# Turning gathered token slices in pairs on two row groups of the matmul engine, and four changes of order beside it

## The chip, the cores and the metric

The kernel runs on one core of a Trainium2 chip. That core has a matmul engine (PE, with its own row for weight loads, PEld), a vector engine (DVE), a scalar engine (ACT), a general engine (POOL) and a queue engine (SP). The metric is the device time of one execution in microseconds (us). All times here are of that one core.

## The reference

Two layers follow each other on x, 16 batches of 128 tokens with 512 features.

```
x = x + attention(layernorm(x), ctx, ctx)      # 32 query heads, 8 key heads, 16 wide, 128 keys
h = layernorm(x)                               # 2048 tokens of 512
tidx, tw = gate(h)                             # 32 experts in 8 groups; best 4 groups, best 8 experts
routed = sum over the 8 chosen experts e of tw[e] * (silu(h @ w1[e].T) * (h @ w3[e].T)) @ w2[e].T
shared = (silu(h @ sw1.T) * (h @ sw3.T)) @ sw2.T      # inner width 256, as each expert
x = x + routed + shared
```

All arithmetic on tokens is fp32.

## The kernel before, in words

The program is one stream of instructions per engine, in an order that is written out by hand: within each engine instructions run in the order in which the Python code emits them, and waits between engines follow from the data and from the memory banks that the tiles share. There are four stages.

**Attention** (lines 272 to 630). There are 32 items, one for each batch and each parity of key heads. An item's `scores` (line 423) are matmuls of 32 rows in four row groups of PE, `values` (line 442) are matmuls of 32 columns in four column groups, and `added` (line 457) turns the result back and adds it to x on POOL. `queries(b)` (line 411) turns one batch's queries on PE and copies them on DVE. Work beside the items hangs on two tables, `head` and `tail`, by item number: layernorm statistics on DVE, reciprocal roots on POOL (`first_rstd`), the masked keys of the next four batches on POOL (`keys`, lines 344 to 350), their values (`fixed_values`, `values_of`). `gate_parts` and `gate_sums` compute the gate's logits. At the end the first of the shared expert's up matmuls fill gaps on PE (`shared_up`, line 246). One shared up is eight matmuls of 512 columns into two PSUM banks: one is read by ACT's silu (line 261), the other by a product on DVE (line 264). An fp32 matmul appears as two records in the trace, a transpose as one.

**Routing** (`route`, line 1033). DVE works out from the logits which experts each token takes (`sel`, line 1129). PE then counts tokens for each expert and ranks them (lines 1137 to 1216). PE has shared up matmuls as cover: `up_matmuls(20)` ahead of the choice, 4 and 9 behind the ranks. Three products of the cover, named `product`, `product0` and `product1`, sit at chosen places in DVE's order. The cover's accumulators come from the pool `ps_gu`, [...].

**The table of tokens** (lines 1289 to 1329). For each of the 16 batches DVE, POOL and ACT build one-hot tiles (`hr`, `hq`, `ht`; two buffers each) and PE multiplies them into `tok`, the list of token numbers for 138 slices of 128 places. Between them PE runs the rest of the shared ups, two matmuls for each batch, and the shared expert's 16 `shared_down`s (two fp32 matmuls each); DVE adds each of these to x (`add_down`) in the `meanwhile` part of the next batches, after that batch's one-hot tiles.

**The experts** (lines 1334 to 1513). The 138 slices are laid one after another, expert after expert, and cut into 52 pieces of at most 512 places. `gather(j)` fetches slice j from DRAM with an indirect DMA that POOL issues, five slices ahead. `turn(j)` (line 1368) transposes the slice on PE, four transposes of 128 x 128 into one bank of `ps_x` (two buffers), and ACT copies it into `xnT` (line 1374). Each piece has four steps. A step is one `up` (four fp32 matmuls, line 1395), then some turns of slices that the next piece needs, then some `down`s (two fp32 matmuls, line 1449; where a slice holds the end of one expert and the start of the next it is done in column groups of 32 or 64). After `down(j)` ACT scales the result (line 1458) and POOL issues an indirect DMA that adds it to the output (line 1421). The loop at lines 1505 to 1509 spreads turns and downs over the four steps:

```
left = 4 - step
for _ in range(-(-turns_left // left)):
    turn_next()
    turns_left -= 1
for _ in range(-(-len(downs_left) // left)):
    down(downs_left.pop(0))
```

Of the kernel before, what the change touches and what calls it, by code (L numbers as in the profile page):

```python
# [9 lines left out]
F32 = mybir.dt.float32  # L10
# [5 lines left out]
PSUM = bass.MemoryType.PSUM  # L16
DRAM = bass.MemoryType.DRAM

P = 128
# [27 lines left out]
def tile_xattn_moe(  # L47
# [15 lines left out]
    nc = tc.nc  # L63
    B, S, D = x.shape
    E, _, ND, I = w1.shape
    NI = I // P
    KV = D // HD // G
    NT = B
    NTB = NT // 4
# [5 lines left out]
    NS = begins[E] // P  # L75
# [6 lines left out]
    ident = const.tile([P, P], F32, name="ident")  # L82
# [189 lines left out]
    def attention_small():  # L272


        with ExitStack() as ph:
# [23 lines left out]
            for half, eng in enumerate((nc.sync, nc.scalar)):  # L299
                rows_of_half = slice(half * P // 2, (half + 1) * P // 2)  # L300
# [217 lines left out]
            def at_head(n, f, *a):  # L518
                head.setdefault(n, []).append((f, a))
# [17 lines left out]
            for b in range(3, B):  # L537
                at_head(2 * b - 3, rows_of, b)

            at_head(1, fixed_values, 1, nc.gpsimd)  # L540
            at_head(1, keys, 1)
            at_head(2, values_of, 1)
            for k in range(2, NTB):
                at_head(8 * k - 7, keys, k)
                at_head(8 * k - 6, values_of, k)
# [27 lines left out]
            for n in range(N):  # L573
                for f, a in head.get(n, ()):
                    f(*a)

                scores(*items[n])
                if n > 0:
                    values(*items[n - 1])
                if n in parts:  # L580
                    gate_parts(parts[n])
                if (n == 1 or n % 2 == 0 and n > 0) and n // 2 + 1 < B:
                    queries(n // 2 + 1)
                keep_warm(FILL.get(n, 0))
                if n in sums:
                    gate_sums(sums[n])
                if n > 1:
                    added(*items[n - 2])
                if n in turned:
                    gate_turn(turned[n], ps_tr)  # L590
                for f, a in tail.get(n, ()):
                    f(*a)
# [365 lines left out]
    def experts(ups, in_order, later, products):  # L958
# [33 lines left out]
        )  # L992
        token2 = wp.tile([P, E - 1], I32, name="token2")
        ps_y = ctx.enter_context(tc.tile_pool(name="ps_y", bufs=2, space=PSUM))
        ps_gu = ctx.enter_context(tc.tile_pool(name="ps_gu", bufs=2, space=PSUM))
        ps_rt = early.enter_context(tc.tile_pool(name="ps_rt", bufs=1, space=PSUM))
        ps_sm = early.enter_context(tc.tile_pool(name="ps_sm", bufs=2, space=PSUM))
        oh = early.enter_context(tc.tile_pool(name="oh", bufs=2))
# [34 lines left out]
        def route():  # L1033
# [70 lines left out]
            for t in range(NT):  # L1104
                nc.vector.max(t8[:, t, :], ms[:, t, :])
                nc.vector.match_replace(rp[:, t, :], t8[:, t, :], ms[:, t, :], LOWEST)
                if t == NT // 2:
                    product1()
                if t == NT // 2 + 1:


                    ranked_p = new([E, 4], "ranked_p")
                    diag = new([E, E], "diag")
                    for i in range(4):
                        nc.vector.scalar_tensor_tensor(
                            diag,
                            ranked[:, i // 2, i % 2 : i % 2 + E],
                            1.0,
                            ident[0:E, 0:E],
                            ALU.mult,  # L1120
                            ALU.mult,
                            accum_out=ranked_p[:, i : i + 1],
                        )
                    rise = new([E, 2], "rise", F16)
                    nc.vector.tensor_tensor(
                        rise, ranked_p[:, 1::2], ranked_p[:, 0::2], ALU.subtract
                    )
# [34 lines left out]
            nc.vector.tensor_scalar(less, size, size_p, None, ALU.is_lt)  # L1162
            sm = new([P, NT], "sm")
            nc.vector.tensor_reduce(sm, comb, AX.X, ALU.add)

            rank = ps_rt.tile([P, NT, E], F32, tag="rank", name="rank")
            nc.tensor.matmul(rank, lhsT=before, rhs=sel, start=True, stop=False)
# [124 lines left out]
        for b in range(NT):  # L1292

            meanwhile = later + held
            held = list(products)
            if b > NT - NTB:
                meanwhile += held
                held.clear()
            later.clear()
            products.clear()  # L1300
            slot_tokens(
                b,
                sr,
                sq,
                slice_q,
                tok,
                oh,
                lambda k: nc.gpsimd if k % 4 == 3 else nc.vector,
                meanwhile,
            )  # L1310
            if b == 2:
                weights()
            if b == 6:
                flags()
            up_matmuls(2)

            for _ in range(b % 2 if b < NT - NTB else 2 if b < NT - 1 else 1):
                shared_down(next(downs))
        finish_tokens(token, tok, oh)
        for f in later + held:  # L1320
# [11 lines left out]


        ps_gu2 = ctx.enter_context(tc.tile_pool(name="ps_gu2", bufs=2, space=PSUM))
        ps_x = ctx.enter_context(tc.tile_pool(name="ps_x", bufs=2, space=PSUM))
        tp = ctx.enter_context(tc.tile_pool(name="tp", bufs=3))
        pieces = []
        for k in range(E):
# [26 lines left out]
            )  # L1365
            xg[j] = t

        def turn(j):
            t = xg.pop(j)
            tr = ps_x.tile([P, ND, P], F32, tag="trx", name="trx")  # L1370
            for d in range(ND):
                nc.tensor.transpose(tr[:, d, :], t[:, ts(d, P)], ident)  # L1372
            for n, a, b, col in parts(j):
                nc.scalar.copy(xnT[n % NTB][:, :, col : col + b - a], tr[:, :, a:b])  # L1374

            ks = [pieces[n][0] for n, *_ in parts(j)]
            by = owner[:, ks[0] : ks[0] + 1] if ks[0] == ks[-1] else owner2[:, ks[0] : ks[0] + 1]
            own = tp.tile([P, E], F32, tag="own", name="own")
            nc.vector.scalar_tensor_tensor(  # L1379
                own, expert, by, t[:, D:], ALU.is_equal, ALU.mult, accum_out=wt[:, j : j + 1]  # L1380
            )
            if ks[0] != ks[-1]:
                k = ks[0]
                nc.vector.tensor_tensor(
                    token2[:, k : k + 1], token[:, j : j + 1], outside[:, k : k + 1], ALU.add
                )
# [91 lines left out]

        def turn_next():
            nonlocal n_turned, n_gathered  # L1480
            if n_gathered < NS:
                gather(n_gathered)
                n_gathered += 1
            turn(n_turned)
            n_turned += 1

        def slices_of(n):

# [5 lines left out]
        for n in range(len(pieces)):  # L1494
            tasks = []
            whole = slices_of(n - 1)[1] if n else 0
            needed = slices_of(n + 1)[0] if n + 1 < len(pieces) else NS
            downs_left = list(range(n_down, whole))
            turns_left = needed - n_turned
            n_down = whole  # L1500
            banks = {}
            for step in range(4):
                up(n, step // 2, step % 2, banks)
# [6 lines that stand above are left out]
# [75 lines left out]
```

## Time and profile before

| | us |
|---|---|
| median of 3 runs | 1013.0 (1012.27 to 1016.13) |
| profiled execution, its own time | 1011.92 |
| its span | 1010.1 |
| PE busy in the span | 987.3 (98%) |
| PE weight loads | 574.8 |
| POOL busy | 512.7 |
| ACT busy | 325.8 |
| DVE busy | 253.3 |
| 552 transposes of gathered slices on PE (line 1372) | 82.9, 273 ns mean of one |
| 150 copies of turned slices on ACT (line 1374) | 81.5, 551 ns mean of one |

The span runs from the first to the last instruction of the core; some 1.8 us of the execution's own time lie around it. The busy time of PE counts a matmul from its start to its modelled end. Matmuls overlap, so the mean of one is longer than the distance from one start to the next, and the distance is what one costs. The granted clock of PE is 0.996 over the span.

### The profile page before, as it was taken

To read this page: it belongs to the slowest core of one execution; us is meant where nothing else is said; L and a number is where in the kernel's file an instruction comes from. 1 tells how busy PE (TensorE), PEld (TensorE's weight loads), DVE (VectorE), ACT (ScalarE), POOL (GpSimd) and SP (SyncE) were. 2 spreads that over 40 slices of the span, in tenths; PEclk is the share of its full clock that TensorE was granted. 3 is DMA by queue.
4 is the path that set the end of the run, shared out by engine and by line. 5 is a ranking of instruction groups with operands and counts; after the bars stand their busy time and mean duration, and the time that the engine had idled before them with its cause. 6 is when DMAs were issued, how large, how long until landed. Compare 5 with 4: busy or idle time off the path is not lost.

```text
span 1010.1 us, 12452 instructions
## 1 busy us (share of the span) xinstructions
PE 987.3 (98%) x4177; PEld 574.8 (57%) x4177; DVE 253.3 (25%) x901; ACT 325.8 (32%) x517; POOL 512.7 (51%) x658
## 2 busy tenths in 40 slices
PE   9999998999999999999999999999999999999996
PEld 5344444547566556676767676767654444444453
DVE  7887668961011000111111111111101000101000
ACT  5666612422222222232323232323232222222221
POOL 5588633754445445554545454545463444554443
PEclk9999999999999999999999999999999999999998
DMA  9011105135666757775757575757575777675643
GB/s 308 8 43 52 54 22 188 52 110 158 158 145 153 160 134 167 167 166 128 188 127 186 127 186 127 187 126 186 129 179 119 169 173 180 142 150 139 124 66 45
DMA packets 59864, 137.06 MB, mean 136 GB/s; under 512 B 12168, under 2 KB 16392, under 8 KB 59792
## 3 DMA queue, kind: packets, MB, share of 16 engines
q0 software_dynamic: 32032, 69.25, 36.3%
q1 hardware_dynamic: 27680, 66.81, 19.9%
q8 instruction: 35, 0.57, 0.2%
q14 instruction: 37, 0.30, 0.1%
q10 hardware_dynamic: 80, 0.13, 0.0%
HBM read 96.71 MB, written 46.73 MB: 142 GB/s over the span
## 4 chain that ended last, share of the span: by engine, by line
PE 76%; POOL 10%; issue 7%; DVE 4%; DMA 2%; ACT 0%; POOLq 0%; DVEq 0%; ACTq 0%
PE gu L1395 44%; PE y L1449 21%; PE trx L1372 6%; PE gu L253 3%; POOL hq L938 2%; POOL out_dram L1421 2%; POOL xn L217 2%; POOL x L474 1%; DMA out_dram<-yw,token 1%; DVE st L91 1%; PE warm L325 1%; POOL kz L350 1%; DVE oTs L454 1%; PE sc L429 1%; POOL h L113 0%
## 5 line engine op out<-in xcount | busy, mean ns | idle before, releaser
L1395 PE MATMUL gu<-xnT,wup 128*128 128x256 f32 (+27 forms) x1664 | 493.2, 445 | 2.4 <-ACT xnT L1374 1.7
L1395 PEld LDWEIGHTS gu<-xnT,wup 128*128 128x128 f32 x1664 | 313.1, 190 | 193.0 <-issue 132.6
L1421 POOL DMA_INDIRECT out_dram<-yw,token x150 | 235.8, 1572 | 357.7 <-ACT yw L1458 258.4
L1449 PE MATMUL y<-wdn,sa 128*128 128x512 f32 (+2 forms) x672 | 260.1, 594 | 0.0
L1406 DVE TENSOR_TENSOR sa<-sl,gu 128x256 f32<-128x256 f32 (+27 forms) x104 | 52.2, 502 | 690.3 <-PE gu L1395 672.0
L1358 POOL DMA_INDIRECT xg<-rows,token x138 | 145.5, 1054 | 48.4 <-issue 33.3
L1458 ACT ACTIVATE yw<-y,wt 128x512 f32<-128x512 f32 x138 | 94.8, 687 | 179.1 <-PE y L1449 153.7
L1449 PEld LDWEIGHTS y<-wdn,sa 128*128 128x128 f32 (+2 forms) x672 | 92.4, 171 | 72.5 <-issue 71.0
L1374 ACT COPY xnT<-trx 128x512 f32<-128x512 f32 (+3 forms) x150 | 81.5, 551 | 141.6 <-PE trx L1372 131.1
L1404 ACT ACTIVATE sl<-gu 128x256 f32<-128x256 f32 (+27 forms) x104 | 46.7, 449 | 240.5 <-PE gu L1395 234.2
L1372 PEld LDWEIGHTS trx<-ident,xg 128*128 128x128 f32 x552 | 69.0, 141 | 36.2 <-issue 24.0
L1372 PE MATMUL trx<-ident,xg 128*128 128x128 f32 x552 | 82.9, 273 | 0.4 <-DMA xg<-rows,token 0.4
L439 ACT ACTIVATE p<-sc 128x1024 f32<-128x1024 f32 x64 | 62.1, 1021 | 29.1 <-PE sc L429 29.1
L253 PE MATMUL gu<-xnT,sup 128*128 128x512 f32 x128 | 59.5, 602 | 2.5 <-DVE sa L264 1.7
L938 POOL TENSOR_SCALAR hq<-slice_q,sq 128x138 f16<-128x138 f16 x32 | 35.2, 1113 | 39.0 <-DVE sq L1242 22.9
L429 PE MATMUL sc<-qT,kz 32*128 32x512 f32 x256 | 41.6, 639 | 1.1 <-DVE qT L420 0.9
L253 PEld LDWEIGHTS gu<-xnT,sup 128*128 128x128 f32 x128 | 22.7, 190 | 26.0 <-issue 20.9
L445 PE MATMUL oT<-p,va 128*32 128x512 f32 x256 | 34.1, 605 | 1.1 <-DVE oTs L454 1.1
L474 POOL TENSOR_TENSOR x<-x,at 128x256 f32<-128x256 f32 x32 | 23.4, 733 | 21.5 <-DVE at L467 21.5
L1379 DVE SCALAR_TENSOR_TENSOR own<-expert,owner,xg 128x32 f32<-128x32 f32 x138 | 31.8, 247 | 1.2 <-DMA xg<-rows,token 1.2
L936 ACT ACTIVATE ht<-hr,token 128x1024 f16<-128x1024 f16 x16 | 18.3, 1147 | 34.4 <-DVE hr L929 34.4
L1276 PE MATMUL y<-sdn,sa 128*128 128x512 f32 x64 | 29.3, 595 | 0.0
(177 smaller groups left out, 467.1 us busy)
## 6 DMA issues: line engine op xcount, KB each, us to landing
wup<-in_w_dram SPq DMA_DIRECT2D x64, 512.0 KB
wdn<-in_w_dram SPq DMA_DIRECT2D x32, 512.0 KB
rows<-xn SPq DMA_DIRECT2D x16, 256.0 KB
out_dram<-x SPq DMA_DIRECT2D x16, 256.0 KB
x<-in_x_dram SPq DMA_DIRECT2D x15, 256.0 KB
out_dram<-yw,token POOLq DMA_INDIRECT x150
xg<-rows,token POOLq DMA_INDIRECT x138
cTs<-in_cT_dram SPq DMA_DIRECT2D x4, 256.0 KB
```

Of the source, the lines that this page charges most:

```text
L253: nc.tensor.matmul(acc, lhsT=sup[:, w, d, ts(i, P)], rhs=xnT[k][:, d, :], start=(d == 0), stop=(d == ND - 1),)
L429: nc.tensor.matmul(scs[j // 2][:, j % 2], lhsT=kzs[b // 4 % 2][rows, b % 4, i, :], rhs=qTs[b][rows], start=True, stop=True, tile_position= ...
L439: nc.scalar.activation(p, sc, AF.Exp, scale=1.0 / HD**0.5)
L938: engine(k).tensor_scalar(hq[:, k, :], tile_q, sq[:, b, k : k + 1], None, ALU.is_equal)
L1358: nc.gpsimd.indirect_dma_start(out=t, out_offset=None, in_=rows[:, :], in_offset=bass.IndirectOffsetOnAxis(ap=token[:, j : j + 1], axis=0) ...
L1372: nc.tensor.transpose(tr[:, d, :], t[:, ts(d, P)], ident)
L1374: nc.scalar.copy(xnT[n % NTB][:, :, col : col + b - a], tr[:, :, a:b])
L1395: nc.tensor.matmul(acc[:, 0:m], lhsT=wup[k % NW][:, w, d, ts(i, P)], rhs=xnT[n % NTB][:, d, 0:m], start=(d == 0), stop=(d == ND - 1),)
L1406: nc.vector.tensor_tensor(acts[n % NTB][:, i, 0:m], banks[2][:, 0:m], acc[:, 0:m], ALU.mult)
L1421: ins = nc.gpsimd.indirect_dma_start(out=flat, out_offset=bass.IndirectOffsetOnAxis(ap=token2[:, k - 1 : k] if a else token[0:b, j : j + 1 ...
L1449: nc.tensor.matmul(y[c0:c1, :], lhsT=acts[n % NTB][:, i, col : col + c1 - c0], rhs=wdn[pieces[n][0] % NW][:, i, :], start=(i == 0), stop=( ...
L1458: nc.scalar.activation(yws[j], y, AF.Copy, scale=wt[:, j : j + 1])
```

## The change

There are five edits.

1. The turn takes two slices. Each slice's 128 rows are taken as two halves of 64. A half is transposed with `tile_position=(0, 0)` or `(64, 0)`: 64 rows of weights by 128 columns, 64 columns moving, so eight transposes for a slice in place of four. The two halves alternate and write to two banks of one `trx` tile, which now has one buffer of two banks. The copy on ACT reads a whole slice from both banks at once; the two parts of a slice that is shared between pieces are copied half by half. `turn_next` gathers two slices and turns two; the number of turns for a piece is halved, rounded up.
2. In the attention, the values and keys of batches 4 to 7 move from items 1 and 2 to items 3, 4 and 5, and `queries(1)` runs ahead of `values` of item 0 instead of behind it.
3. `ps_gu` is taken from the other end of PSUM.
4. In the routing, `product1` moves from the middle of the choice of experts to behind the sums of the weights.
5. In the table, the last four batches get 2, 1, 1 and 0 shared downs in place of 2, 2, 2 and 1, so six are left for behind the table in place of three.

```diff
@@ attention
-            at_head(1, fixed_values, 1, nc.gpsimd)
-            at_head(1, keys, 1)
-            at_head(2, values_of, 1)
+            at_head(3, fixed_values, 1, nc.gpsimd)
+            at_head(4, keys, 1)
+            at_head(5, values_of, 1)
...
                 scores(*items[n])
+                if n == 1:
+                    queries(1)
                 if n > 0:
                     values(*items[n - 1])
...
-                if (n == 1 or n % 2 == 0 and n > 0) and n // 2 + 1 < B:
+                if n % 2 == 0 and 0 < n // 2 < B - 1:
                     queries(n // 2 + 1)
@@ experts
-        ps_gu = ctx.enter_context(tc.tile_pool(name="ps_gu", bufs=2, space=PSUM))
+        ps_gu = ctx.enter_context(tc.tile_pool(name="ps_gu", bufs=2, space=PSUM, side="right"))
@@ route
-                if t == NT // 2:
-                    product1()
...
             nc.vector.tensor_reduce(sm, comb, AX.X, ALU.add)
+            product1()
@@ table
-            for _ in range(b % 2 if b < NT - NTB else 2 if b < NT - 1 else 1):
+            for _ in range(b % 2 if b < NT - NTB else (NT - b) // 2):
                 shared_down(next(downs))
@@ the turn
-        ps_x = ctx.enter_context(tc.tile_pool(name="ps_x", bufs=2, space=PSUM))
+        ps_x = ctx.enter_context(tc.tile_pool(name="ps_x", bufs=1, space=PSUM))
-        def turn(j):
+        H = P // 2
+        def turn(js):
+            tr = ps_x.tile([P, 2, 2, ND, H], F32, tag="trx", name="trx")
+            for s, j in enumerate(js):
+                for d in range(ND):
+                    for h in range(2):
+                        rows_of_half = slice(h * H, (h + 1) * H)
+                        nc.tensor.matmul(
+                            tr[:, h, s, d, :],
+                            lhsT=xg[j][rows_of_half, ts(d, P)],
+                            rhs=ident[rows_of_half, rows_of_half],
+                            start=True,
+                            stop=True,
+                            is_transpose=True,
+                            tile_position=(h * H, 0),
+                        )
+            for s, j in enumerate(js):
+                turned(j, tr[:, :, s])
+        def turned(j, tr):
             t = xg.pop(j)
-            tr = ps_x.tile([P, ND, P], F32, tag="trx", name="trx")
-            for d in range(ND):
-                nc.tensor.transpose(tr[:, d, :], t[:, ts(d, P)], ident)
             for n, a, b, col in parts(j):
-                nc.scalar.copy(xnT[n % NTB][:, :, col : col + b - a], tr[:, :, a:b])
+                if b - a == P:
+                    nc.scalar.copy(
+                        xnT[n % NTB][:, :, col : col + P].rearrange("p d (h t) -> p h d t", h=2), tr
+                    )
+                    continue
+                for h in range(2):
+                    a0, b0 = max(a, h * H), min(b, (h + 1) * H)
+                    if a0 < b0:
+                        nc.scalar.copy(
+                            xnT[n % NTB][:, :, col + a0 - a : col + b0 - a],
+                            tr[:, h, :, a0 - h * H : b0 - h * H],
+                        )
...
         def turn_next():
             nonlocal n_turned, n_gathered
-            if n_gathered < NS:
-                gather(n_gathered)
-                n_gathered += 1
-            turn(n_turned)
-            n_turned += 1
+            js = range(n_turned, min(n_turned + 2, NS))
+            for _ in js:
+                if n_gathered < NS:
+                    gather(n_gathered)
+                    n_gathered += 1
+            turn(js)
+            n_turned += len(js)
...
-            turns_left = needed - n_turned
+            turns_left = -(-(needed - n_turned) // 2)
```

## The prediction

> **What bounds the kernel now.** I read the busy time of the engines by stage first, because the changes lie in four stages. Columns: length, then busy us and count for PE, PEld, DVE, ACT, POOL, the granted clock, DMA share, GB/s.
>
> ```profile
> 0.00:132.00 132.00, 126.14 (x921) 59.89 (x921) 99.59 (x251) 80.16 (x98) 87.66 (x199) 1.00 0.27 93
> 132.00:172.00 40.00, 35.35 (x130) 16.31 (x131) 30.57 (x131) 7.96 (x11) 13.34 (x143) 1.00 0.21 73
> 172.00:228.00 56.00, 56.00 (x240) 28.22 (x239) 45.41 (x127) 17.64 (x17) 34.72 (x32) 1.00 0.32 110
> 228.00:985.00 757.00, 754.23 (x2830) 460.53 (x2829) 76.53 (x390) 215.84 (x385) 367.73 (x278) 1.00 0.66 151
> ```
>
> PE bounds everything. In the experts' 757 us it stands still for 2.8 us, and no other engine is half full, so a cost there is the distance between PE starts. The routing, 132 to 172 us, has 4.65 us without PE; there a wait is worth its length.
>
> The timeline of PE at one turn (start, length, line):
>
> ```profile
> 528.44 0.60 PE L1372 MATMUL trx<-ident,xg 128*128 128x128 f32 x4
> 528.97 1.92 PE L1449 MATMUL y<-wdn,sa 128*32 128x512 f32 x16
> 530.82 0.69 PE L1395 MATMUL gu<-xnT,wup 128*128 128x252 f32 x2
> ```
>
> and at another, where a full-width down follows:
>
> ```profile
> 503.34 0.60 PE L1372 MATMUL trx<-ident,xg 128*128 128x128 f32 x4
> 503.77 1.88 PE L1449 MATMUL y<-wdn,sa 128*128 128x512 f32 x4
> ```
>
> 503.34 to 503.77 is four transposes: 109 ns each, not the 273 ns of the mean row. Two slices cost 8 x 109 = 872 ns. At 528.44 the down in column groups starts 0.53 us after, 92 ns later than 4 x 109: [...] The way back shows it again: 16 records in groups of four are 4 x 429 = 1.72 us, so the down's data has passed at 530.73, and the next up starts at 530.82; its first weights are not loaded ahead either, so its second record comes 317 ns later where 212 is its pace (105 more).
>
> The nearest row for row groups is the scores of attention, 32 rows in four groups. Weight loads, then matmuls:
>
> ```profile
> 65.53 0.20 PEld L429 LDWEIGHTS sc<-qT,kz 32*128 32x128 f32 x4 [0.17 <-issue]
> 65.53 0.71 PE L429 MATMUL sc<-qT,kz 32*128 32x512 f32 x4
> ```
>
> Four loads of 0.18 us each fit into 0.20 us, and four matmuls of 0.69 into 0.71: row groups load and multiply side by side, some 7 ns apart.
>
> **The turn.** Per pair of slices the change has 16 transposes, 8 for each row group. How fast can one group run? Moving 64 columns takes half of 109, about 56 ns. Its weight load has 128 columns as before. The load's own pace is seen where the moving side is short, the gate sums with 32 columns:
>
> ```profile
> 124.66 0.41 PEld L505 LDWEIGHTS lg<-fold,lgTs 128*128 128x128 f32 x3 [0.22 <-issue]
> ```
>
> Three loads of 0.19 us end after 0.41: 111 ns apart. Those are loads of a multiply; a transpose's load shows 141 ns against 190, about 50 less, so its pace is 58 to 60 ns. I take 59, weight-bound. [...] If the two groups' loads took turns, eight pairs would be 8 x 118 = 944 ns, more than the 872 now; by the scores' row they overlap, and it is 472. The row decides, though it shows 32-row groups.
>
> Around it stand two changes of tiling. [...] In: 92 ns empty. Eight paces with the first load open: 8 x 59, the last stream 56, a stagger of 7. Out: 92 empty and 107 for an open load of an up or down. Sum 92 + 472 + 56 + 7 + 199 = 826 ns against 872: 46 saved. By the drain at nothing it would be 445 saved; with loads in turn, 426 lost. From the loop's arithmetic there are 69 pairs; 58 have full-width work on both sides and one opens the stage, 10 are followed by a down in column groups. Those paid a change anyway (92 + 27 for its small load): 872 + 119 = 991 before, 92 + 472 + 56 + 7 + 119 = 746 after, 245 saved. Sum: 59 x 0.046 + 10 x 0.245 = **5.1 us**. Bounds: one ns of pace is 0.55 us over 552 paces; 53 ns gives 8.4, 70 gives -1.
>
> ACT copies twice per pair, 2 x 0.59 us, before the one `trx` buffer is free. The next pair never follows sooner than one up and usually a down (1.6 to 3.4 us), so I cost the lost buffer at nothing; uncovered, 18 pairs share a piece with another and might wait up to 0.5 us each, 9 us. The 12 split slices add one copy of some 0.3 us each, hidden. POOL's gathers come in twos, 1.0 us each; the scatter behind them waits a microsecond longer, and nothing waits for it. A slice is now fetched at least two pairs, some 20 us, ahead; the first ones land about 5 us after their issue.
>
> **Waits that go with it.** In three pieces the last turn stands in step 4 with no down behind it, and the next up waits for ACT:
>
> ```profile
> 741.41 2.84 PE L1395 MATMUL gu<-xnT,wup 128*128 128x512 f32 x6 [0.68 <-ACT xnT L1374]
> ```
>
> Starts against pace give 0.84, 0.84 and 0.52 us. Pairs finish in steps 1 and 2, so **2.2 us** go.
>
> **Routing.** PE and DVE:
>
> ```profile
> 137.23 17.43 PE L253 MATMUL gu<-xnT,sup 128*128 128x512 f32 x40 [1.71 <-DVE sa L264]
> 151.34 0.69 DVE L264 TENSOR_TENSOR sa<-ssl,gu 128x512 f32<-128x512 f32 x1 [2.67 <-PE gu L253]
> 156.63 0.55 PE L1137 MATMUL count<-ones,sel 128*32 128x1 f16 x16 [1.96 <-DVE sel L1129]
> ```
>
> PE waits 1.71 for `product` because `ps_gu` lies on the banks of attention's scores, where the first shared up is held. At the other end lie the banks of `oT` and `o`, last read near 131 us: the wait goes. DVE waits 2.67 us and works 0.69 for `product1` in the middle of the choice; moved, `sel` comes 3.3 us sooner, and 0.87 more because `product0` no longer waits for a later PE: about 152.4, when PE arrives at 156.63 - 1.96 - 1.71 = 152.96. So PE loses neither wait: 3.67 us gained. `product1` then delays what DVE does behind it by 0.69, of which the rank matmuls hide all but about 0.25 (the place of experts, then the slots, then the silu for which PE already waits 0.75). Net **3.4 us**. If the bank edit fails to free PE, 1.96 remain; the bounds are 1.5 and 3.7.
>
> **Attention's start.** The scores of the third item (item 2) begin with
>
> ```profile
> 15.96 0.71 PE L429 MATMUL sc<-qT,kz 32*128 32x512 f32 x4 [0.91 <-DVE qT L420]
> ```
>
> because `queries(1)` stands behind `values`. Ahead of it, it must wait for DVE's `xq` (14.07 now), [...]. Moved, POOL's 1.1 us of memsets and 3.1 of keys lie at items 3 to 5, before they are read at item 8; the same keys at 42.4 us lengthen no item. They are queued ahead of x's additions, which only statistics two items later await. Gain 0 to 0.9; I take **0.5**.
>
> **The table's end.** DVE's chain, not PE, is near the edge here:
>
> ```profile
> 213.14 0.69 DVE L1286 TENSOR_TENSOR x<-y,x 128x512 f32<-128x512 f32 x1 [1.03 <-PE y L1276]
> 213.74 1.22 DVE L929 TENSOR_TENSOR hr<-slot_r,sr 128x1024 f16<-128x1024 f16 x1
> 215.06 1.15 ACT L936 ACTIVATE ht<-hr,token 128x1024 f16<-128x1024 f16 x1 [6.00 <-DVE hr L929]
> 216.91 0.66 PE L944 MATMUL tok<-hq,ht 128*128 128x138 f16 x8
> ```
>
> PE comes to this `tok` at 216.9, and `ht` was ready at 216.2. With one down fewer (1.72 us) PE would come at 215.1 and stand 1.15; at the last `tok` it would stand another 0.7. Cost **1.8 us** (bounds 0 and 2.5). In return six downs, 10.3 us, cover the first gather in place of four, and 0.54 us of wait for slice 1 goes. The wait for the first copies (0.84) becomes some 1.1. Together **0.3 gained**.
>
> **Sum.** 5.1 + 2.2 + 3.4 + 0.5 - 1.8 + 0.3 = 9.7 us off the profiled execution's 1011.9: 1002.2. That execution lies 1.1 under the median of the runs shown, so I say **1002.5**, a little above it.
>
> **The rivals.**
> Slower, chance 0.08: in 64-row groups the loads take turns, or a load takes the multiply's 111 ns. The pace becomes 111 to 118 instead of 59: 552 x 55 ns = 30 us lost against 9.7 gained, about 1033. Against it stand the scores' loads and the 141 ns of a transpose's load; for it, that no row shows 64 rows. It decides from a pace of 59 + 9.7 / 0.552 = 77 ns.
> The turn gains nothing, 0.12: a pace near 70, or waits for the single `trx` buffer; the other edits leave 3 to 5 us: 1008.
> More than worked out, 0.10: the drain overlaps the loads, 92 ns x 69 = 6.3 us, and the table costs nothing: 995.
> As worked out, 0.70: 998 to 1007.
>
> Half a per cent, 5 us, is about what a measurement can tell from no change. Faster by that: the main case nearly whole, the better case and a third of the even one, 0.83; within it 0.09; slower 0.08. The range 995.5 to 1010 leaves out the slower case and about a tenth more at its ends.
>
> **What would show it.** The transposes of `trx` come as 1104 records, two starts some 7 ns apart and then about 59 until the next two; a start later than 65 proves the load bound wrong. A pair's first start comes 92 ns after the stream ahead has passed. The three waits for `xnT` are gone. No wait before the count, and none at 137 us. Two waits of about a microsecond at the last two `tok` groups. If PE shows waits for ACT before `trx`, the lost buffer counts, and I was wrong there.

## The result, and the profile after

The changed kernel takes **1002.9 us** (median of 4 runs, 1002.80 to 1002.94); beside it the kernel before took 1014.6 (4 runs, 1012.27 to 1016.28). The ratio is 0.9886, 95% interval 0.987 to 0.9901. The forecast was 1002.5, range 995.5 to 1010. The profiled execution of the changed kernel took 1002.89 us, its span is 1001.1: 9.0 us under the profiled execution of before (1011.9), where the sum of the prediction had 9.7.

Where the time went, by the starts of single PE instructions in the two profiled executions (us):

| stretch of PE's time | before | after | difference | prediction |
|---|---|---|---|---|
| start to the last gate sum (`lg`): attention | 132.59 | 133.32 | +0.73, of it +0.22 start | -0.5 |
| to the first `count`: choice | 24.04 | 20.03 | -4.01 | -3.67 |
| to the first `tok`: slots | 15.75 | 15.87 | +0.12 | +0.25 |
| to the first `trx`: table | 55.93 | 57.65 | +1.72 | +1.8 |
| to the first expert `gu`: first turn | 2.32 | 1.91 | -0.41 | -0.3 |
| to the end: experts | 779.51 | 772.34 | -7.17 | -7.3 |

Experts, routing and table came out within half a microsecond of their terms. Attention has the wrong sign: beside the start, which came 0.22 us later, it lost 0.51.

The timeline of PE in the changed kernel, at the places whose lines the prediction showed of before (start, length, line, operation, shape, count; in brackets an idle time ahead and what ended it):

```profile
15.25 1.14 PE L429 MATMUL sc<-qT,kz 32*128 32x512 f32 x8
...
133.43 19.99 PE L253 MATMUL gu<-xnT,sup 128*128 128x512 f32 x46
153.35 0.55 PE L1138 MATMUL count<-ones,sel 128*32 128x1 f16 x16
...
213.11 0.67 PE L946 MATMUL tok<-hq,ht 128*128 128x138 f16 x8 [0.90 <-ACT ht L938]
215.92 0.67 PE L946 MATMUL tok<-hq,ht 128*128 128x138 f16 x8 [0.37 <-ACT ht L938]
226.87 0.71 PE L1380 MATMUL trx<-ident,xg 64*128 64x64 f32 x16
228.78 1.56 PE L1427 MATMUL gu<-xnT,wup 128*128 128x256 f32 x6 [1.20 <-ACT xnT L1396]
```

The scores of item 2 begin 0.7 us sooner. From 133.43 on PE runs without a stop into the count: both waits of the choice are gone. At the last two `tok` groups it now stands, as forecast. The sixteen half transposes of a pair take 0.71 us; before, each of two slices had a row of 0.60. The waits of PE in the changed kernel, summed (total, times, longest):

```profile
PE oT L445 <- DVE oTs L454: 2.5, 3, 1.2
PE tok L946 <- ACT ht L938: 1.3, 2, 0.9
PE gu L1427 <- ACT xnT L1396: 1.2, 1, 1.2
```

The three waits for `xnT` inside the experts are gone; the 1.2 us is the very first pair. At `oT` there were two waits of 1.1 us together before; that they are 2.5 us now is attention's loss. And busy time by stage in the changed kernel (columns as in the prediction's table):

```profile
158.00:168.00 10.00, 9.25 (x23) 3.88 (x22) 8.52 (x39) 3.48 (x4) 4.79 (x4) 1.00 0.71 266
228.00:985.00 757.00, 756.22 (x3402) 445.37 (x3403) 76.38 (x388) 214.07 (x398) 367.53 (x277) 1.00 0.65 151
```

In the experts PE now stands still for 0.8 us of 757. The same clock, 1.00, runs in both kernels, so nothing of the 7.17 is a matter of clock.

One turn in the trace of after: two starts 3 to 4 ns apart, one of each row group, then the next two. The distances between starts are 3, 109, 3, 59, 3, 59, 3, 59, 4, 61, 4, 60, 3, 58, 4 ns, and 151 ns from the last start to the next operation. That gives 643 ns in that turn (the median of all is 640). Ahead of it lie 94 ns: from the last start of the matmul of 512 columns ahead to the first start of the turn it is 523 ns, where 429 is the pace. Behind it the second start of the next full-width down comes after 533 ns in place of 429, 104 more. The transposes of one group follow each other every 62 ns (59 + 3), the first two after 112.

### The profile page after: what moved, and what is told of

Same layout as the page of the kernel before. It is cut to its first block, busy times and chain, and to the rows that moved or that the text cites. A ratio compares the mean times of both kernels' runs of the same rounds, so it can differ in the third digit from the quotient of the medians.

```text
span 1001.1 us, 13488 instructions
## 1 busy us (share of the span) xinstructions
PE 981.6 (98%) x4729; PEld 554.0 (55%) x4729; DVE 252.3 (25%) x901; ACT 322.5 (32%) x526; POOL 512.2 (51%) x658
## 4 chain that ended last, share of the span: by engine, by line
PE 71%; issue 2%; POOL 2%; DMA 1%; POOLq 0%; ACT 0%
PE gu L1427 44%; PE y L1481 23%; PE trx L1380 4%; POOL out_dram L1453 2%; DMA out_dram<-yw,token 1%; ACT sl L1436 0%; POOLq L1453 0%; POOLq L1554 0%
## 5 line engine op out<-in xcount | busy, mean ns | idle before, releaser
L1481 PE MATMUL y<-wdn,sa 128*128 128x512 f32 (+2 forms) x672 | 265.7, 603 | 0.0
L1481 PEld LDWEIGHTS y<-wdn,sa 128*128 128x128 f32 (+2 forms) x672 | 96.1, 170 | 87.4 <-issue 77.3
L1396 ACT COPY xnT<-trx 128x512 f32<-128x512 f32 x126 | 68.3, 589 | 66.3 <-PE trx L1380 66.0
L1380 PEld LDWEIGHTS trx<-ident,xg 64*128 64x128 f32 x1104 | 39.6, 138 | 33.6 <-issue 33.6
L1380 PE MATMUL trx<-ident,xg 64*128 64x64 f32 x1104 | 49.0, 229 | 0.0
L1411 DVE SCALAR_TENSOR_TENSOR own<-expert,owner,xg 128x32 f32<-128x32 f32 x138 | 29.4, 247 | 0.0
```

What stands on the lines that cost most here:

```text
L1380: nc.tensor.matmul(tr[:, h, s, d, :], lhsT=xg[j][rows_of_half, ts(d, P)], rhs=ident[rows_of_half, rows_of_half], start=True, stop=True, is ...
L1396: nc.scalar.copy(xnT[n % NTB][:, :, col : col + P].rearrange("p d (h t) -> p h d t", h=2), tr)
L1481: nc.tensor.matmul(y[c0:c1, :], lhsT=acts[n % NTB][:, i, col : col + c1 - c0], rhs=wdn[pieces[n][0] % NW][:, i, :], start=(i == 0), stop=( ...
```

## The experiments

There are twelve runs. Where nothing else is said, an edit is made to the changed kernel, and a difference is against its 1002.9 us. Differences of stages are between profiled executions, by PE's starts as in the table above.

**1. The turn alone.** The kernel before with `turn`, `turned`, `turn_next` and the single `trx` buffer of the change, and nothing else of it.

> The kernel before with the paired turn alone. Theory: the turn is worth what the experts' stage lost, 7.2 us from the first up to the end (779.5 to 772.3), and a little at the first turn: 1004.5 us profiled, and routing (132.2 us to the count at 156.6) as before. Rival, that the edits of order carry most of it: 1009 or more.

Measured: 1009.7 us (1009.25 to 1010.77), ratio 0.9965 (0.9953 to 0.9978). That is the rival's number, but not its reason: the experts gained their 7.17 us with the turn alone. The ratio is worth only 3.5, because two stages gave the rest back. First, slots: +3.19 us. Windows of this kernel, and then of before:

```profile
158.00:168.00 10.00, 10.00 (x32) 4.95 (x31) 8.16 (x41) 1.33 (x2) 2.13 (x2) 0.66 0.27 101
```

```profile
158.00:168.00 10.00, 9.25 (x38) 4.31 (x36) 9.29 (x42) 2.33 (x3) 3.33 (x3) 1.00 0.41 134
```

The granted clock, the third value from the end, is 0.66: in this stretch the clock stood at half for 6.83 us, from 158.7 us on. No instruction differs here from before; only the clock does. All six runs show a mean clock of 0.993 or 0.994, so the profiled one is no exception. The second stage is the first turn, +1.63 us: a pair needs slices 0 and 1, which the four downs of the old table don't cover. PE's timeline in this kernel:

```profile
233.19 0.46 PE L1379 MATMUL trx<-ident,xg 64*128 64x64 f32 x8 [1.04 <-DMA xg<-rows,token]
...
235.63 1.56 PE L1426 MATMUL gu<-xnT,wup 128*128 128x256 f32 x6 [1.98 <-issue]
```

What follows: the turn is worth what its term said, but the kernel keeps the gain only in company of the edits that take away PE's stands ahead of the count and at the first turn.

**2. All but the turn.** The old `turn` with two `trx` buffers; the other edits stay.

> The changed kernel with the turn of before (one slice, four full-width transposes, two buffers). Theory: 1002.9 + 7.2 = 1010.1 us: the four edits of order are worth 2 us together (routing 4.0 gained, table 1.7 and attention 0.7 lost, the first gather's wait 0.5 gained). The experts' stage is 779 us as before. Rival, that the edits of order carry the change: 1004 to 1006.

Measured: 1009.6 us (1009.60 to 1010.01), ratio 0.9963 (0.9949 to 0.9977). As expected; choice -4.00, experts as before. The full transposes stand again at their old cost.

**3. Pairs, but full width.** Two slices per turn, each by four transposes of 128 rows (shortened; the layout of `trx` and the copy on ACT follow):

```
-                    for h in range(2):
-                        nc.tensor.matmul(tr[:, h, s, d, :], ..., tile_position=(h * H, 0))
+                    nc.tensor.transpose(tr[:, s, d, :], xg[j][:, ts(d, P)], ident)
```

> The changed kernel, slices still turned in pairs at the same places, but by eight full-width transposes of 128 rows in place of sixteen of 64. Theory: the three waits for the copies stay away (2.2 us), and the row groups' own 36 ns for each pair with full-width work behind it and 235 ns for each of the ten with a down in column groups behind it are lost: 59 x 0.036 + 10 x 0.235 = 4.5 us, so 1007.4. Rival, that the groups only break even with their drains and the places of the turns are the gain: 1003.

Measured: 1007.4 us (1007.31 to 1007.43), ratio 0.9942 (0.9926 to 0.9959). As expected. Of the 7.17 us in the experts 2.71 come from turning in pairs, which places the turns, and 4.46 from the row groups. The group of `trx` in the lists of instructions, this kernel and then the changed one:

```profile
L1374 PE MATMUL trx<-ident,xg 128*128 128x128 f32 x552 | 71.5, 273 | 0.0
```

```profile
L1380 PE MATMUL trx<-ident,xg 64*128 64x64 f32 x1104 | 49.0, 229 | 0.0
```

Over 69 pairs that is 1.04 us against 0.71 per pair, the overlapped ends included. The busy row says 22.5 us less; the time moved by 4.5. The rest, some 0.29 us for a pair between full-width work, is in part the overlapped ends (0.16 us of a pair at full width, 0.07 of one in row groups) and for the rest the two changes of tiling (94 + 104 ns), which lie between the `trx` rows and their neighbours and in nobody's busy time.

**4. First one half, then the other.** Eight transposes of the upper 64 rows and then eight of the lower, in place of alternating:

```
-            for s, j in enumerate(js):
-                for d in range(ND):
-                    for h in range(2):
+            for h in range(2):
+                for s, j in enumerate(js):
+                    for d in range(ND):
```

> The changed kernel with the sixteen transposes of a pair in another order: the eight of rows 0 to 63 first, then the eight of rows 64 to 127, so that neighbours lie in the same row group. Theory (the gain of the row groups is that the loads of two groups overlap): 16 paces of 59 ns instead of 8, 69 x 0.47 = 32 us more, 1035. Rival (the pace is set by the transposes' issue or by something the order doesn't touch): 1003.

Measured in one run: 1023.7 us, 20.8 more. Neither number was met. The group:

```profile
L1380 PE MATMUL trx<-ident,xg 64*128 64x64 f32 x1104 | 70.0, 229 | 0.0
```

21.0 us more in 69 pairs, 0.305 each. Inside one half the starts are 62 ns apart, so the pace of one group is the same; in the middle of every turn, three starts follow the one ahead after 5 to 8 ns, where the second half runs beside the rest of the first. So 8 paces became 13, not 16: three of the sixteen transposes still ran beside another. What follows: the gain of the row groups here is the overlap, and the order of issue makes it (20.8 us without it).

**5. Row groups, but one slice per turn.**

```
-            js = range(n_turned, min(n_turned + 2, NS))
+            js = range(n_turned, min(n_turned + 1, NS))
...
-            turns_left = -(-(needed - n_turned) // 2)
+            turns_left = needed - n_turned
```

> The changed kernel with one slice for each turn, still in two row groups. Theory: 69 turns more, each with its own change of tiling in and out, 94 + 50 + 56 + 60 + 104 = some 366 ns, 25 us, and the three waits for copies come back, 2.2 us: 1030. So single turns in row groups would be slower than the kernel before. Rival (a change of tiling costs next to nothing once loads can run ahead): 1005.

Measured in one run: 1028.6 us, as expected within 1.4. One slice takes 391 ns to the next operation where a full-width one takes 4 x 109 = 436, and pays the 94 ns ahead and the 104 of the open load behind as well. With 69 more pairs of tiling changes the kernel is 25.7 us slower, 0.37 each, and slower than before the change. The pairing is not a detail of the row groups; it is what makes them pay.

**6. The memsets back at item 1.**

```
-            at_head(3, fixed_values, 1, nc.gpsimd)
+            at_head(1, fixed_values, 1, nc.gpsimd)
```

> The changed kernel with the values' memsets of batches 4 to 7 back at item 1; the keys stay at item 4 and the copy at item 5. Theory: the memsets, 1.1 us ahead of the first additions to x on POOL, make DVE's statistics late, and with them the copies that PE waits for at the items 6 and 8; both waits go (0.55 and 0.93 us), 1001.5. Rival, that the 3.4 us of keys in front of the next addition are the cause: items 6 and 8 stay longer by more than 0.9 together, 1002.5 or more.

Measured: **1001.7 us** (1001.68 to 1001.82), ratio 0.9887 to its runs of before (0.987 to 0.9903). It is as expected, 1.2 under the changed kernel, and the fastest of all that ran. Item 2 keeps its 0.92, and what items 3 to 12 lost falls from 1.49 to 0.43. The lines of POOL and DVE in the changed kernel show how:

```profile
25.64 0.95 POOL L353 MEMSET va<- 128x1024 f32 x1
26.73 0.72 POOL L474 TENSOR_TENSOR x<-x,at 128x256 f32<-128x256 f32 x1
...
27.49 0.69 DVE L91 BATCH_NORM_STATS2 st<-x 128x6 f32<-128x512 f32 x1 [1.74 <-POOL x L474]
```

```profile
29.49 1.06 PE L445 MATMUL oT<-p,va 128*32 128x512 f32 x8 [0.47 <-DVE oTs L454]
...
37.02 1.07 PE L445 MATMUL oT<-p,va 128*32 128x512 f32 x8 [1.16 <-DVE oTs L454]
```

POOL sets memory while x's addition stands behind it; DVE's statistics wait 1.74 us for that addition; the copy of `oTs` stands behind the statistics on DVE, and PE waits for it. With the memsets back, the same addition starts 1.3 us sooner:

```profile
25.45 0.73 POOL L474 TENSOR_TENSOR x<-x,at 128x256 f32<-128x256 f32 x1
```

**7. All three POOL and DVE steps back.** `fixed_values`, `keys` and `values_of` at items 1, 1 and 2 as before; `queries(1)` stays ahead of `values`.

> The kernel after with fixed_values, keys and values of the second block of slots back at items 1, 1 and 2; queries(1) stays ahead of values. Theory from the run with the memsets alone put back: items 3 to 12 get all of their 1.49 us back, but item 2 loses a part of its 0.93, because POOL's keys slow DVE's xq again (0.55 against 0.43 us) and DVE's are queued behind it. Net of the two between -1.3 and -0.3 us against the kernel after: 1001.6 to 1002.6. If the keys at item 4 cost nothing and the memsets were the whole, it is 1001.7 as with these alone; [...]

Measured: 1002.8 us (1002.58 to 1003.14), ratio 0.9898 (0.9881 to 0.9914). That is 0.2 above the range, and the inner split was not as expected: item 2 loses all of its 0.92, not a part. PE's timeline:

```profile
14.44 0.66 PE L416 MATMUL tr<-ident,xq 128*128 128x128 f32 x4 [0.90 <-DVE xq L394]
```

So the earlier queries alone only move the wait from `qT` to `xq`. DVE in this kernel, and then in the changed one:

```profile
13.18 0.62 DVE L110 SCALAR_TENSOR_TENSOR rstd<-h,r 128x3 f32<-128x3 f32 x1
13.83 0.55 DVE L394 TENSOR_SCALAR xq<-x,mv,rstd 128x512 f32<-128x512 f32 x1
```

```profile
12.87 0.16 DVE L110 SCALAR_TENSOR_TENSOR rstd<-h,r 128x3 f32<-128x3 f32 x1
13.07 0.55 DVE L394 TENSOR_SCALAR xq<-x,mv,rstd 128x512 f32<-128x512 f32 x1
```

`xq` itself takes 0.55 us in both. Two short operations ahead of it take 0.61 and 0.62 us while POOL works on the keys (10.10 to 13.22 us), and 0.16 without them, and `xq` begins 0.76 us later. That the two take longer beside POOL's work on the keys is shown; why is not. The 0.92 of item 2 needs both edits, the keys gone and the queries earlier; the keys' move alone did not run. The 0.43 lost in items 3 to 12 stays here too, with every POOL step at its old place, so it goes with `queries(1)`, the one edit of attention left. The three parts, in this order of taking back: keys -0.92, memsets +1.06, queries +0.43.

**8. gu's banks back on the old side**, `side="right"` taken away.

> The changed kernel with the pool of the up accumulators back on the banks of attention's scores. Theory: PE waits 1.7 us again for the first product near 135 us, and nothing else: 1004.6. The run with the turn alone showed the granted clock at half for 6.8 us behind the count, where PE had stood twice. If one of the two waits is enough for that, the granted clock falls in some runs and these are 2 to 3.5 us longer, 1006.6 to 1008.

Measured: 1004.9 us (1004.86 to 1005.22), ratio 0.9914 (0.9897 to 0.9931). As expected: the wait of 1.7 us at 137 us is there again, the count comes 1.97 us later, and there is no wait before the count. No stretch at half clock follows.

```profile
137.84 17.43 PE L253 MATMUL gu<-xnT,sup 128*128 128x512 f32 x40 [1.70 <-DVE sa L264]
155.21 0.55 PE L1138 MATMUL count<-ones,sel 128*32 128x1 f16 x16
```

**9. product1 back in the middle of the choice**, the banks stay.

> The kernel after with product1 back in the middle of the choice; the banks of gu stay on the new side. Theory of the prediction: the choice ends one multiply (0.69 us) and its wait later; with the banks moved the wait of product1 for PE is shorter than the 2.67 us of before, since PE no longer stands 1.71 us. PE meets its wait before the count again, 1.5 to 2.0 us; the slots gain back some 0.25. So the count about 1.9 us later than in the kernel after, the whole 1004.5 (1004 to 1005). One single stand of PE should leave the granted clock at full, as it did with the banks alone put back. Rival, from the run with the banks put back (count 1.97 us later): each of the two edits alone is worth nearly nothing more than its own wait, so the two sums 2.0 + 2.0 make the whole 4.0; were they dependent, this run would show 3 us or more, or under 1.

Measured: 1007.3 us (1006.30 to 1008.26), ratio 0.9938 (0.9922 to 0.9955). The count is 2.03 us later as expected, so the two edits of the choice are worth 2.0 each and add up. But the slots took 3.0 us more, which was not expected: in the profiled execution the clock stood at half for 6.83 us again, after a single stand of 1.96 us before the count:

```profile
155.61 0.55 PE L1140 MATMUL count<-ones,sel 128*32 128x1 f16 x16 [1.96 <-DVE sel L1132]
```

```profile
158.00:168.00 10.00, 10.00 (x30) 5.01 (x29) 8.20 (x40) 1.74 (x2) 3.15 (x3) 0.69 0.39 124
```

Of the four runs two took 1008.2 and 1008.3 us at a mean clock of 0.994, and two 1006.3 and 1006.4 at 0.996. Behind the stand of 1.70 us at 137 us, with full work on both sides, the clock stayed at 1.00 (8); behind this one of 1.96 us before the count, which sixteen small f16 matmuls of one column and the thinly filled ranks follow, it fell. It did not always: the profiled execution of before has the same 1.96 us and kept its clock, 1.00. What the traces show of the difference stands in the next section.

**10. The old division of the shared downs in the table**, 2, 2, 2, 1 in place of 2, 1, 1, 0:

```
-            for _ in range(b % 2 if b < NT - NTB else (NT - b) // 2):
+            for _ in range(b % 2 if b < NT - NTB else 2 if b < NT - 1 else 1):
```

> The changed kernel with the shared downs of the table as before (2, 2, 2, 1). By the prediction's sum the edit costs 1.8 us and returns 0.3, so without it 1001.4. By the stages of the run with the turn alone, the paired turn needs two gathered slices at its first turn and waits 1.0 us for the second one and 2.0 for the copies when no downs cover it, 2.0 us more than the changed kernel from the first transpose to the first up; then the edit pays for itself in company of the paired turn: 1003.2.

Measured: 1006.7 us (1006.23 to 1007.03), ratio 0.9929 (0.9912 to 0.9946): 3.8 slower, where both forecasts said about even or faster. The table stage gave its 1.6 us back: the last `tok` comes 1.82 later, and from there the first turn 3.43 sooner. But then (PE's timeline, and below it ACT's):

```profile
226.28 0.46 PE L1380 MATMUL trx<-ident,xg 64*128 64x64 f32 x8 [0.67 <-DMA xg<-rows,token]
230.68 3.78 PE L1427 MATMUL gu<-xnT,wup 128*128 128x256 f32 x8 [3.94 <-issue]
```

```profile
229.55 1.07 ACT L1396 COPY xnT<-trx 128x512 f32<-128x512 f32 x2 [12.62 <-remote]
```

The first turn to the first expert `gu` takes 5.53 us instead of 1.91. PE waits 0.67 for slice 1, and ACT's copies begin 2.8 us after the last transpose. The release for which ACT waits is PE's own, and it comes at 229.53 us in this trace; so it is PE's release that came late, and why is not settled. Eight `gu` records, 1.99 us in the kernel before, take 3.78 us: the clock stood at half for 6.83 us, from 228.44 us on, and that costs 2.15 more. 1.82 - 3.43 + 3.61 + 2.15 = 4.15, the 4.1 us between the spans.

**11. The two edits of the choice alone**, in the kernel before.

> The kernel before with the two edits in the routing alone: gu's banks on the other side and product1 behind the choice. The count comes 4.00 us sooner, as in every kernel that has both, and the slots give 0.12 back: against the fastest times of before (1012.1 to 1012.7) 3.9 less, 1008.3 to 1008.8. The disputed point is the spread. Theory: the executions of before above 1013 are those in which the granted clock is halved behind the wait for the count; without that wait the runs agree within 0.6 us and the median is 1008.5, some 5 us under before's median. Rival: before's spread has another cause (the first gather, the loads of the weights); then these runs spread over 2 us as before's do, with a median near 1010.

Measured: 1009.2 us (1008.23 to 1010.95), ratio 0.9964 (0.995 to 0.9978). The choice gained 4.00 and the slots gave 0.12 back, as in the changed kernel, without the turn. The disputed point went to the rival: the runs spread over 2.7 us, four of them within 1.2 us and one at 1010.95. The trace, of the run of 1009.19, shows no stretch at half clock. In this trace the excess is at the first turn, which takes 3.03 us where it took 2.32:

```profile
226.49 0.66 PE L1371 MATMUL trx<-ident,xg 128*128 128x128 f32 x4 [1.10 <-DMA xg<-rows,token]
```

**12. The kernel before once more.**

> The kernel before, unchanged, for one more trace of it. Theory of the halved clock: if this execution takes over 1013 us, its records show the granted clock at half in some stretch between 158 and 168 us, and the first tok comes later than 172.4 by the excess over 1012.1; if it takes under 1013, they show full speed there. Rival: an execution over 1013 with the full clock between 158 and 168 us, its excess at another place.

Measured in one execution: 1013.6 us, clock 1.00 between 158 and 168 us. The theory of the halved clock falls for this one. The wait for slice 1 here, and then in the trace that the prediction used:

```profile
230.89 0.66 PE L1372 MATMUL trx<-ident,xg 128*128 128x128 f32 x4 [1.40 <-DMA xg<-rows,token]
```

```profile
229.29 0.66 PE L1372 MATMUL trx<-ident,xg 128*128 128x128 f32 x4 [0.39 <-DMA xg<-rows,token]
```

The stage from the first `trx` to the first `gu` is 1.01 us longer here, every later stage is equal to a hundredth, and the rest of the excess (0.6 us) was there before the third item of attention. From the end of slice 1's issue on POOL to the end of PE's wait it is 5.05 us here and 4.04 there. So the landing of the first gathers varies from run to run, and with four downs ahead of it PE pays for the variation. With six it does not: the runs of the changed kernel lie within 0.14 us of each other.

## Why the prediction was right, and where it was not

The time was right, 1002.5 against 1002.9, and most terms with it; three things were wrong. That it came so close is in part luck: attention's term was off by 1.0 us beside the start, and the surplus of the routing and the 0.3 us added for the median took more than half of that back.

- **The turn: right.** 46 ns for a pair between full-width neighbours was 36 in the trace: 94 ahead, 640 to the next operation and 104 for its open load, so 838 against the old event of 874. The period of one group is 62 ns, not 59, and the first one 112; the stagger is 3 to 4 ns, not 7. One side sum of the prediction does not come out: with both 92 ns and the open load at nothing it would be 337 ns saved, not 445. Turn and waits for `xnT` together gave 7.17 us against 5.1 + 2.2; the run with pairs at full width splits them 4.46 and 2.71. The lost `trx` buffer costs nothing that a wait shows. That the loads overlap at 64 rows too was the author's estimate, from the row of the scores with its 32, and it was right. A load of 64 rows lasts 138 ns in the changed kernel (median) against 141 of 128 rows before, so it is the overlap, not a shorter load, that pays. The rival of loads in turn, a pace of 118 ns, fell with the 62. The run with the halves in turn shows what the order of issue costs when few starts overlap, 0.305 us per pair and not the 8 x 59 = 0.472 of no overlap at all.
- **Routing: right, slightly undersized.** 3.67 for two waits became 4.01. A stop costs PE more than its wait. At 137 us it is 0.27 us more (run 8): the last matmul ahead runs out for 0.59 us where its successor would have started after 0.43, and behind the stop the second start comes 0.10 later than the pace (in the trace of before the first weight load starts there at 137.23 us, together with the matmul, and not ahead of it). Ahead of the count it is 0.07 (run 9), because the count starts 0.52 us after the last matmul even without a wait. The loss behind it was 0.12, not 0.25. The two edits add up, 2.0 each.
- **The table: the term was right, its return was not.** 1.8 us lost was 1.72, partly by luck: the two waits are 1.27 of it, where the prediction had 1.15 and 0.7; each of the two stops costs 0.16 beyond its wait, and the 94 ns ahead of the first turn lie in this stretch. In return 0.3 was expected and 0.41 measured between the two traces; but without the edit the paired turn costs 4.1 us more in the trace. The step that failed is "six downs, 10.3 us, cover the first gather in place of four, and 0.54 us of wait for slice 1 goes": it priced the wait by one execution of before, whose wait is the shortest of the three traced with the old turn and the old table (0.39, 1.10 and 1.40 us), and took the pair's second slice, ACT's copies and the clock for free. The expectation of run 10 repeated that mistake.
- **Attention: wrong in sign.** 0.5 us gained was forecast, 0.51 lost was measured beside the shift of the start. "They are queued ahead of x's additions, which only statistics two items later await" failed: the statistics that wait for x stand in DVE's queue ahead of the `oTs` copy of the next item, so 1.06 us of POOL's 1.1 arrive at PE. Another 0.43 came with the earlier queries, for which the prediction had no cost. That the 0.55 us of `xq` is the keys' doing, for which they were moved, was the author's estimate, and run 7 refutes it: `xq` takes 0.55 without them too. What takes longer beside them are two short operations ahead of it (0.61 and 0.62 us against 0.16). The gain of 0.92 was there, at the upper end of the term's bounds 0 to 0.9.
- **Left out: the clock.** The prediction used full clock all through. That held for before and after as profiled, up to 1002.98 and 995.77 us (half from there to the end), but runs 1, 9 and 10 lose 2.15 to 3.2 us each to a stretch at half:

```profile
155.28:158.69 3.41, 1.98 (x38) 1.31 (x38) 2.84 (x11) 0.11 (x1) 0.00 (x0) 1.00 0.00 0
158.69:165.52 6.83, 6.83 (x23) 3.58 (x23) 5.06 (x31) 0.59 (x1) 0.00 (x0) 0.50 0.05 12
```

These are the lines of run 1, columns as before. In each of the 14 traces all changes of the granted clock lie whole multiples of 3.413 us apart: the full clock lasts 292 of them in before and 290 in the changed kernel, the stretch of run 1 two. Where they fall differs from execution to execution: the next such place ahead of the count is 1.4 us ahead in run 1 (155.28, the count 156.72) and 0.2 in before (156.47, 156.63). So each trace can be laid out in windows of 3.413 us. Counted in the time that PE's matmuls take to move their columns (0.84 ns a column in f32 and 0.41 in f16, by their paces of 429 and 210 ns for 512 columns), some windows of the traces held this much:

| window, us | stand in it | columns moved in it | clock after it |
|---|---|---|---|
| run 10, 225.03 to 228.44 | 2.37 | 0.88 | half |
| run 9, 153.98 to 157.39 | 1.63 | 1.09 | half |
| run 1, 155.28 to 158.69 | 1.44 | 1.15 | half |
| run 12, 135.89 to 139.30 | 1.72 | 1.43 | full |
| before, 153.06 to 156.47 | 1.81 | 1.44 | full |
| run 1, 233.79 to 237.20 | 1.84 | 1.46 | full |

The length of the stand does not order these rows; the columns do. Of 4083 windows at full clock in the 14 traces, 17 are followed by half, these three and one at the end of each kernel, and none of the 17 held more than 1.15 us of columns; no other held less than 1.43. That is what these traces hold; no run tried a value between the two, and what makes the clock fall is not shown. In runs 1 and 9 it is the count and the ranks behind the stand that leave the window so little. Before has the same stand ahead of the count as run 1 (1.96 us); there a window ended at 156.47 us, just ahead of the count at 156.63, and parted the stand from the thin work. If such windows are slid over the trace of before, some 6 of 10 positions have one of at most 1.15 us and 7 one under 1.43; over that of the changed kernel none has. This last is an estimate from the two traces; the windows were not moved by an experiment.
- **The median.** The prediction said that the profiled execution of before lies 1.1 us under its median, and added only 0.3 for it. The changed kernel's profiled execution lies at its median, so side by side the medians lie 11.7 us apart and the two profiled executions 9.0. Run 12 shows a part of the 2.7 us between, the wait for slice 1. Another part goes with the clock: of 32 further executions of before, the 17 over 1013.6 us all have a mean granted clock of 0.994 to 0.996, and 12 of the 15 below have 0.997 or 0.998. A mean of 0.996 alone proves nothing, since the traced execution of before has it without such a stretch, and no trace of one of the 17 is kept; so where their clock fell is not shown.

## What to carry to other kernels

Row groups paid here by overlap: alternate them in the order of issue (20.8 us in run 4), and put enough work into one event that the change of tiling ahead and behind (here 94 + 104 ns) is a small part of it; against pairs at full width, two slices per turn gained 4.5 us and one slice lost some 21 (25.7 - 4.5). Remove a stand of PE ahead of thin matmuls even where the profiled execution shows only its length: behind 1.96 us ahead of the count two traces (runs 1 and 9) have 6.83 us at half clock, and two of before have none. An edit that only hides a transfer looks worthless in an execution where the transfer came early (0.39 us of wait here, against 1.10 and 1.40 in two others): judge it by several executions, and with the edits beside it, since their gains need not add. A step moved in an idle engine's queue was paid by what stands behind it there, one consumer further than the author looked (1.06 of POOL's 1.1 us reached PE).

## What the runs showed of the hardware that was not expected

Two groups of 64 rows start 3 to 4 ns apart, and the next two follow 59 ns later, 62 ns from start to start in one group; issued in blocks instead, only three of sixteen starts fall beside another, 5 to 8 ns behind it. The granted clock falls to half for 6.83 us inside three kernels (from 158.7 us on in run 1), and costs 2.15 to 3.2 us each time. In each of the 14 traces its changes lie on a grid of 3.413 us; behind windows with at most 1.15 us of moved columns it fell, behind those with 1.43 or more it did not, and nothing between was met. The second gathered slice, for which PE waits at the first turn, lands 1.0 us later after its issue in one execution of the same kernel than in another (5.05 against 4.04). And a stop of PE costs 0.07 to 0.27 us beyond the wait that the records show, by what stands on both sides of it.
